# Attention's group norm: squares about the group's mean on ScalarE in place of VectorE's statistics

## The chip, the cores and the metric

The kernel runs on one core of a Trainium2 chip. The metric is the time of one execution on the device in microseconds, the median of several runs. The traces come from single executions, recorded by the hardware profiler.

## The reference

The whole program is four layers on images `x` of 32 x 192 x 56 x 56 in fp32; each layer adds its result to `x`. The change touches the first layer only, an attention with 49 "agent" tokens for each image, in six heads, on a group-normed input:

```python
def _gn(v, G=32, eps=1e-5):            # groups of 6 channels
    g = v.reshape(B, G, C // G, H, W)
    m = mean(g, axis=(2, 3, 4)); s = var(g, axis=(2, 3, 4))
    return ((g - m) / sqrt(s + eps)).reshape(v.shape)

# layer 0, on _gn(x)
qkv = xf @ Wqkv + bqkv                              # q, k, v; 3136 tokens, 192 channels
agent = q in 7 x 7 blocks of 8 x 8 pixels, averaged  # 49 tokens
agent_attn = softmax(agent * scale @ k^T + pos_bias) # over the 3136 tokens
agent_v = agent_attn @ v
q_attn = softmax(q * scale @ agent^T + agent_bias)   # over the 49 agents
out = (q_attn @ agent_v + depthwise_conv3x3(v)) @ proj_w + proj_b
x = x + out
```

The other three layers (a two-way recurrent scan, a shift with a 3 x 3 filter, a long convolution through spectra) come after it and are not changed.

## The kernel before

`all_blocks` builds a filter for the last layer (`make_filter`), runs `attention` image by image, then `scan_pairs` and `channel_blocks`. Attention takes the first 4,990 us of the profiled execution.

An image lies in SBUF as two tiles with channels in the partitions: `x[0]` holds channels 0 to 127 as 128 x 3136, and `x[1]` holds the other 64 channels as 128 x 1568, the upper half of the picture in partitions 0 to 63 and the lower half in 64 to 127. The picture is cut into `NK` = 4 vertical strips of `WIDTHS` 16, 16, 16 and 8 columns; `j` counts strips.

The loop over images has two halves. In the first half, for each strip, `weigh` makes agents' scores (L659, L660), their negative maximum `low` on VectorE (L661) and their exp on ScalarE (L663); `turn_v`, `turn`, `gather` and `settle` transpose and sum them with v; `find_v` makes v for a later strip, `convolve` its depthwise filter on VectorE (eight L646 for each of two tiles). With the last strip, `moments` of the *next* image is called. In the second half, `join` combines the strips (L724 to L739). Then `ask(j)` scores pixels against agents (products L751 and L752, maximum L755, difference L756, exp L764 on ScalarE, row sums L766 to L768), `turn_back` transposes the result (L778) and ScalarE copies it out of PSUM as `pqT` (L782), `answer` multiplies by the agents' values (L791, L796, added by L793 and L797), and `project` multiplies by `proj_w` (L911 to L924) and adds to the image (L806, L812), with a square for the next layer's norm (L819). These are staggered over `t`:

```python
for t in range(1, NK + 2):
    if t < NK:            asked[t] = ask(t, gq)
    if more and t == 1:   mean, d = spread_of(mv)
    if more and t == 2:   rs, nb = scaling(mean, d, pools); normed(nxt, rs, nb, 0)
    if t <= NK:           back[t - 1] = turn_back(t - 1, asked[t - 1])
    ...
    if t >= 2:            project(t - 2, done[t - 2], x, st)
    if t <= NK:           answer(t - 1, back[t - 1], values, done[t - 1])
```

The norm of the next image is spread over these steps. `moments` takes, on VectorE, seven `bn_stats` of 448 elements for `x[0]` (L512) and four of 392 for `x[1]` (L514), two aggregates (L516, L517) that give mean and variance of each partition, then sums of eight neighbours `by_x` (L521) and from those the 7 x 7 block sums `pool_a` and `pool_c` (L524 to L535). `grouped` forms sums over the six channels of a group with four small TensorE products (L542). `spread_of` gets the group's mean from them and `d`, the partition's variance plus the square of its distance from the group's mean. `scaling` takes the group's mean of `d`, makes `rs` and `nb` (Ln and Exp on ScalarE, L560 and L561), and scales the block sums. `normed` writes the normed strips (L599, L603) and `find_agents` makes the agents from the block sums (L575).

All PSUM work in attention uses one pool of four tiles of two banks; a product that begins a new tile waits for the reader of the one that it takes. `pr` (L662) and `pqT` (L781) share five buffers with the tag `weights`. The order of instructions on each engine is made by the scheduler of the framework when the program is built, not by the order of the source alone; on the chip each engine goes through its own list in order.

Of the kernel before, what the change touches and what calls it, by code (L numbers as in the profile page):

```python
# [20 lines left out]
F32 = mybir.dt.float32  # L21
I32 = mybir.dt.int32
AF = mybir.ActivationFunctionType
ALU = mybir.AluOpType
AX = mybir.AxisListType
# [5 lines left out]
S = 56  # L31
N = S * S
CH = 448
# [8 lines left out]
AG = 49  # L42
POOL = 7
PAIR = 2 * AG
# [189 lines left out]
def make_filter(ctx: ExitStack, tc: tile.TileContext, a, consts, filt, lags, spans, taps, beside):  # L234
# [9 lines left out]
    FE, FO = a["L3_conv_W1T"].shape  # L244
    P2 = KS * KS
    RC = 5
    n = RC * KS

    def load(name, shape, ap):
# [4 lines left out]
    w1 = load("w1", [FE, FO], a["L3_conv_W1T"])  # L254
    z = load("z", [FE, P2], a["L3_conv_z"].rearrange("b c h w -> (b c) (h w)"))
    ws = load("ws", [128, 128 + C + 4], a["filter_w"])
# [4 lines left out]
    dist = load(  # L261
        "dist", [T, P2], a["L3_conv_distance_map"].rearrange("a b h w -> (a b h w)").partition_broadcast(T)
    )
# [174 lines left out]
def attention(ctx: ExitStack, tc: tile.TileContext, a, ready, x1, st_a, st_c, beside):  # L438
# [9 lines left out]
    nc = tc.nc  # L448
    NB = x1.shape[0]
    cp = ctx.enter_context(tc.tile_pool(name="a_c", bufs=1))  # L450
    wp = ctx.enter_context(tc.tile_pool(name="a_w", bufs=2))
# [3 lines left out]
    UP, LOW = slice(0, 64), slice(64, 128)  # L455
    HALVES = ((0, UP), (1, LOW))
    P2 = slice(0, PAIR)

    def psum():
        return pp.tile([128, 2, BANK], F32, name="ps", tag="ps")  # L460
# [30 lines left out]
    def small(name, shape):  # L491
        return sp.tile(shape, F32, name=name, tag=name)
# [13 lines left out]

    def moments(x):

        st_a, st_c = small("st_a", [128, 7, 6]), small("st_c", [128, 4, 6])
        flat = [t.rearrange("p y x -> p (y x)") for t in x]  # L510
        for i in range(7):
            nc.vector.bn_stats(st_a[:, i], flat[0][:, i * 448 : (i + 1) * 448])  # L512
        for i in range(4):
            nc.vector.bn_stats(st_c[:, i], flat[1][:, i * 392 : (i + 1) * 392])  # L514
        mv = small("mv", [128, 2, 2])
        nc.vector.bn_aggr(mv[:, 0], st_a.rearrange("p a b -> p (a b)"))  # L516
        nc.vector.bn_aggr(mv[:, 1], st_c.rearrange("p a b -> p (a b)"))  # L517
        pool_a, pool_c = small("pool_a", [128, AG]), small("pool_c", [65, AG])
        by_x = [wp.tile([128, n, POOL], F32, name="by_x", tag=f"by_x{n}", bufs=1) for n in (S, S // 2)]
        for t in range(2):  # L520
            nc.vector.tensor_reduce(  # L521
                by_x[t].rearrange("p y q -> p (y q)"), x[t].rearrange("p y (q x) -> p (y q) x", x=8), AX.X, ALU.add
            )
        nc.vector.tensor_reduce(  # L524
            pool_a.rearrange("p (w q) -> p w q", w=POOL), by_x[0].rearrange("p (w y) q -> p w q y", y=8), AX.X, ALU.add
        )
        fours = small("fours", [64, 2 * POOL, POOL])
        for h, r in HALVES:
            nc.vector.tensor_reduce(
                fours[:, h * POOL : (h + 1) * POOL], by_x[1][r].rearrange("p (w y) q -> p w q y", y=4), AX.X, ALU.add  # L530
            )
        nc.vector.tensor_tensor(
            pool_c[0:64].rearrange("p (w q) -> p w q", w=POOL), fours[:, 0::2], fours[:, 1::2], ALU.add
        )
        nc.vector.memset(pool_c[64:65], 1.0)  # L535
        return mv, (pool_a, pool_c)

    def grouped(src):
        ps = psum()
        for t in range(2):  # L540
            for s in range(2):
                mm(ps[:, 0, t : t + 1], norm4[:, 2 * s + t], src[s], start=(s == 0), stop=(s == 1))  # L542
        return ps[:, 0, 0:2]

    def spread_of(mv):

        mean = small("mean", [128, 2])
        nc.vector.tensor_copy(mean, grouped([mv[:, t, 0:1] for t in range(2)]))
        d = small("d", [128, 2])
        nc.vector.tensor_tensor(d, mv[:, :, 0], mean, ALU.subtract)  # L550
        nc.vector.tensor_tensor(d, d, d, ALU.mult)
        nc.vector.tensor_tensor(d, d, mv[:, :, 1], ALU.add)
        return mean, d

    def scaling(mean, d, pools):
# [95 lines left out]
    def weigh(j, g, low, sums):  # L651
        _, n, _ = sizes(j)
        prs = []
        for p in range(3):
            cols = slice(p * PAIR, (p + 1) * PAIR)
            ps = psum()
            for h in range(2):
                px = slice(h * n, (h + 1) * n)
                mm(ps[P2, h, :n], g[:, cols], xs_a[j][:, px], start=True, stop=False)  # L659
                mm(ps[P2, h, :n], gk_c[0:KC, 2 * j + h, cols], xs_c[j][0:KC, px], start=False, stop=True)  # L660
            nc.vector.tensor_reduce(low[:, j, p : p + 1], ps[P2, :, :n], AX.XY, ALU.max, negate=True)  # L661
            pr = wp.tile([PAIR, 2, CH], F32, name="pr", tag="weights", bufs=5)  # L662
            nc.scalar.activation(  # L663
                pr[:, :, :n], ps[P2, :, :n], AF.Exp, bias=low[:, j, p : p + 1], accum_out=sums[:, j, p : p + 1]
            )
            prs.append(pr)
        return prs
# [103 lines left out]
    def turn_back(j, pq):  # L771
        _, n, ns = sizes(j)
        out = []
        for p in range(3):
            ps = psum()
            for q in range(2 * ns):
                h, s = divmod(q, ns)
                nc.tensor.transpose(  # L778
                    ps[P2, h, s * SUB : (s + 1) * SUB], pq[:, q, p * PAIR : (p + 1) * PAIR], ident[:SUB, :SUB]
                )  # L780
            t = wp.tile([PAIR, 2, CH], F32, name="pqT", tag="weights", bufs=5)  # L781
            nc.scalar.copy(t[:, :, :n], ps[P2, :, :n])  # L782
            out.append(t)
        return out
# [38 lines left out]

    nxt = ready.first
    mv, pools = moments(nxt)
    rs, nb = scaling(*spread_of(mv), pools)
    ag = find_agents(0, pools)
    gk = seen(ag, wkT, gk_c, "gk_a")
    for j in range(NK):
# [3 lines left out]
    for b in range(NB):  # L833
        x, more = nxt, b + 1 < NB
        if more:
            nxt = ready.image(nc, a, b + 1)
        beside(b)
        low, sums = small("low", [PAIR, NK, 3]), small("sums", [PAIR, NK, 3])
        got = sp.tile([PAIR, NK, C], F32, name="got", tag="got", bufs=1)
        turned, asked, back = {}, {}, {}  # L840
        for j in range(NK):
            prs = weigh(j, gk, low, sums)
            if j == 0:
                gq = seen(ag, wqT, gq_c, "gq_a")
            vT = turn_v(j, v[j])
            if j > 0:
                halves = gather(j - 1, *turned[j - 1])
            if j + 2 < NK:
                v[j + 2] = find_v(j + 2)
            turned[j] = turn(j, prs), vT  # L850
            if j > 0:
                settle(j - 1, halves, got)
            if j + 1 < NK:
                o[j + 1] = convolve(j + 1)
            elif more:
                mv, pools = moments(nxt)
        halves = gather(NK - 1, *turned[NK - 1])
        asked[0] = ask(0, gq)
        settle(NK - 1, halves, got)
        values = join(low, sums, got)  # L860
        done, o = o, {}
        st = small("st", [128, 2, 9])
        for t in range(1, NK + 2):
            if t < NK:
                asked[t] = ask(t, gq)
            if more and t == 1:
                mean, d = spread_of(mv)
            if more and t == 2:
                rs, nb = scaling(mean, d, pools)
                normed(nxt, rs, nb, 0)  # L870
            if t <= NK:
                back[t - 1] = turn_back(t - 1, asked[t - 1])
            if more and t in (3, 4):
                v[t - 3] = find_v(t - 3)
            if t >= 2:
                project(t - 2, done[t - 2], x, st)
            if t <= NK:
                answer(t - 1, back[t - 1], values, done[t - 1])
            if more and t == 2:
                ag = find_agents(b + 1, pools)  # L880
                normed(nxt, rs, nb, 1)
            if more and t == 3:
                gk = seen(ag, wkT, gk_c, "gk_a")
                normed(nxt, rs, nb, 2)
            if more and t == 4:
                o[0] = convolve(0)
                normed(nxt, rs, nb, 3)
        nc.sync.dma_start(out=st_a[:, b % 2, b // 2], in_=st[:, 0])
        for h, r in HALVES:
            nc.sync.dma_start(out=st_c[b % 2, :, h, b // 2], in_=st[r, 1])  # L890
        nc.sync.dma_start(out=x1[b, 0:128], in_=x[0].rearrange("p y x -> p (y x)"))
        for h, r in HALVES:
            nc.sync.dma_start(
                out=x1[b, 128:C, 1568 * h : 1568 * h + 1568], in_=x[1][r].rearrange("p y x -> p (y x)")
            )
# [1082 lines left out]
```

## Time and profile before

| | |
|---|---|
| median of 3 runs | 10,783.73 us (10,777.28 to 10,800.41) |
| the profiled execution | 10,811.08 us, its span 10,809.3 us |
| granted TensorE clock, mean of the span | 0.95 |
| busy of the span: TensorE, VectorE, ScalarE, GpSimd | 89%, 86%, 59%, 27% |
| attention, join of the first image to join of the last (L727) | 256.4 to 4,910.8 us, 31 intervals |
| join to join, images 2 to 23 | 150.0 to 151.6 us |
| L512, 224 executions | 0.61 us (median) |
| L514, 392 elements | 0.55 us |
| L819, 896 elements with its sum | 1.04 us, and 0.19 to read the sum |

Times in traces are counted from the start of the span. In the timelines a row has start, length, engine, line and operation, the tiles it writes and reads with partitions x elements, and how many like rows were put together; in brackets stands how long the engine sat idle before it and what ended that. L12 is line 12 of the kernel before. PE is TensorE, PEld its weight loads, DVE VectorE, ACT ScalarE, POOL GpSimd, SP SyncE. The windows view gives busy time of each engine in a stretch, the clock that TensorE was granted there (1.00 is full), and the DMA engines' share.

### The profile page before, as it was taken

How to read it: one execution, taken by the hardware profiler on the slowest of the kernel's cores; microseconds unless marked ns; L12 is line 12 of the kernel's file. 1: busy time of each engine (PE TensorE's matmuls, PEld its weight loads, DVE VectorE, ACT ScalarE, POOL GpSimd, SP SyncE). 2: the span in 40 equal slices, each digit the busy share in tenths (PEclk: the TensorE clock that was granted, in tenths of full speed). 3: DMA queues.
4: the chain of work that ended last, by engine and by line, in shares of the span. 5: the costliest groups of instructions: out<-in, count | busy, mean ns of one | idle time of the engine just before them, and what ended most of it. 6: DMA issues, size and time to landing. Idle time of an engine off the chain costs nothing. (4 is left out here: it accounts for less than half of the span.)

```text
span 10809.3 us, 166766 instructions
## 1 busy us (share of the span) xinstructions
PE 9604.3 (89%) x64806; PEld 5959.0 (55%) x64806; DVE 9260.0 (86%) x11668; ACT 6372.8 (59%) x11964; POOL 2918.0 (27%) x2614
## 2 busy tenths in 40 slices
PE   6999999999999999998888888888888799999998
PEld 3555555555555555554333333333333577787876
DVE  5888888888888888887999999999999577777877
ACT  3555555555555555554666666666666466666766
POOL 0000000000000000002655555555555444444441
PEclk8999999999999999998999999999999899999999
DMA  4211221112121111111344333333444589999998
GB/s 122 63 47 49 63 64 63 37 58 63 64 63 35 61 46 46 46 34 56 92 102 98 97 97 97 97 97 97 97 101 103 153 269 273 274 275 273 278 274 264
DMA packets 1104877, 1240.31 MB, mean 115 GB/s; under 512 B 773091, under 2 KB 807200, under 8 KB 1091992
## 3 DMA queue, kind: packets, MB, share of 16 engines
q1 hardware_dynamic: 1083148, 1201.53, 38.8%
q10 hardware_dynamic: 20932, 28.02, 1.0%
q8 instruction: 516, 8.45, 0.3%
q14 instruction: 281, 2.30, 0.1%
HBM read 915.94 MB, written 306.43 MB: 113 GB/s over the span
## 5 line engine op out<-in xcount | busy, mean ns | idle before, releaser
L646 DVE SCALAR_TENSOR_TENSOR o<-v_a,att_w,o 128x896 f32<-128x896 f32 (+1 forms) x1024 | 1053.3, 1029 | 421.7 <-ACT v_a L620 296.6
L1163 POOL MEMSET f<- 128x1 f32 x96 | 8.8, 98 | 4842.7 <-DMA st_c<-st 4837.7
L1543 DVE STREAM_TRANSPOSE z<-turned 128x1792 f32<-128x1792 f32 x192 | 677.4, 3528 | 258.3 <-ACT turned L1543 257.8
L1543 ACT COPY y<-ps 64x252 f32<-64x252 f32 (+1 forms) x2304 | 784.0, 340 | 157.9 <-PE ps L1543 128.1
L1156 ACT ACTIVATE q<-q 128x784 f32<-128x784 f32 x384 | 328.3, 855 | 813.6 <-DVE q L1151 638.5
L663 ACT ACTIVATE pr<-ps,low 98x896 f32<-98x896 f32 (+1 forms) x384 | 352.3, 918 | 567.8 <-DVE low L661 567.8
L911 PE MATMUL ps<-sq,fixed 128*128 128x392 f32 x512 | 296.8, 742 | 427.7 <-ACT sq L1234 427.7
L764 ACT ACTIVATE pq<-pq 112x1176 f32<-112x1176 f32 x224 | 265.3, 1184 | 683.3 <-DVE pq L756 654.1
L751 PE MATMUL ps<-gq_a,xs_a 128*112 128x294 f32 x1792 | 609.0, 422 | 46.6 <-DVE pq L756 24.1
L1543 POOL TENSOR_TENSOR xn<-x,scale 128x896 f32<-128x896 f32 x192 | 328.4, 1711 | 1192.3 <-DMA x<-x 759.4
L646 DVE SCALAR_TENSOR_TENSOR o<-v_c,att_w,o 128x448 f32<-128x448 f32 (+1 forms) x1024 | 634.3, 619 | 7.5 <-ACT v_c L631 2.4
L659 PE MATMUL ps<-xs_a,gk_a 128*98 128x448 f32 (+1 forms) x1536 | 638.9, 497 | 0.0
L660 PE MATMUL ps<-xs_c,gk_c 125*98 125x448 f32 (+1 forms) x1536 | 631.3, 492 | 0.0
L911 PE MATMUL ps<-x,weights 128*128 128x392 f32 x1536 | 573.7, 516 | 31.1 <-DVE bv L1185 14.1
L752 PE MATMUL ps<-gq_c,xs_c 125*112 125x294 f32 x1792 | 581.4, 411 | 0.0
L1543 PEld LDWEIGHTS ps<-toep,y 128*32 128x32 f32 x16896 | 508.2, 151 | 113.4 <-ACT y L1543 109.2
L1543 PE MATMUL ps<-toep,y 128*32 128x112 f32 x16896 | 554.8, 287 | 0.0
L1543 PE MATMUL ps<-rows,xn 128*112 128x112 f32 x3072 | 378.5, 281 | 159.6 <-POOL xn L1543 136.0
L1543 ACT ACTIVATE turned<-ps,rs 128x448 f32<-128x448 f32 (+1 forms) x576 | 384.4, 668 | 203.4 <-PE ps L1543 195.7
L1543 PE MATMUL ps<-fixed,padded 128*128 128x168 f32 x3072 | 490.0, 314 | 0.0
L766 DVE TENSOR_REDUCE sm<-pq 112x24 f32<-112x1176 f32 x224 | 307.7, 1374 | 181.9 <-ACT pq L764 181.9
L1543 PEld LDWEIGHTS ps<-fixed,padded 128*128 128x128 f32 x3072 | 455.6, 195 | 2.4 <-issue 1.9
(367 smaller groups left out, 25548.6 us busy)
## 6 DMA issues: line engine op xcount, KB each, us to landing
toep<-spans SPq DMA_DIRECT2D x192, 2352.0 KB
x<-x SPq DMA_DIRECT2D x576, 392.0 KB
x<-x SPq DMA_DIRECT2D x896, 196.0 KB
out_x<-done SPq DMA_DIRECT2D x384, 196.0 KB
spans<-lags SPq DMA_DIRECT2D x24, 2352.0 KB
x<-in_x SPq DMA_DIRECT2D x32, 1568.0 KB
x<-x SPq DMA_DIRECT2D x32, 1568.0 KB
x<-in_x SPq DMA_DIRECT2D x64, 392.0 KB
```

What stands on the lines that cost most here:

```text
L646: nc.vector.scalar_tensor_tensor(dst, tap(i), dww[:, t, i : i + 1], dst, ALU.mult, ALU.add)
L659: mm(ps[P2, h, :n], g[:, cols], xs_a[j][:, px], start=True, stop=False)
L660: mm(ps[P2, h, :n], gk_c[0:KC, 2 * j + h, cols], xs_c[j][0:KC, px], start=False, stop=True)
L663: nc.scalar.activation(pr[:, :, :n], ps[P2, :, :n], AF.Exp, bias=low[:, j, p : p + 1], accum_out=sums[:, j, p : p + 1])
L751: mm(ps[:SUB, i, :HA], xs_a[j][:, px], g, start=True, stop=False)
L752: mm(ps[:SUB, i, :HA], xs_c[j][0:KC, px], gq_c[0:KC, 2 * j + (q + i) // ns], start=False, stop=True)
L764: nc.scalar.activation(flat, flat, AF.Exp)
L766: nc.vector.tensor_reduce(sm, rows, AX.X, ALU.add)
L911: mm(out, aa, srcs[t][h], start=True, stop=False)
L1156: nc.scalar.activation(den, den, AF.Ln)
L1163: nc.gpsimd.memset(s, 0.0)
L1543: return lambda *args, **kw: self.tc.keep_in_program_order(do(*args, **kw))
```

## The change

The statistics instructions leave `moments`. It sums `by_x` once more to get each partition's sum (`mv`). `spread_of` now takes the image as well: it scales the sums to means, gets the group's mean, and has ScalarE take squares of the image about it, six activations of 784 elements, each with its sum in `parts`. VectorE adds the parts and scales them to `d`. The squares themselves are not used; they are written to buffers of the `weights` tag. `scaling`, `normed` and what follows are as before. The first image, whose norm is made ahead of the loop, takes the same path.

```diff
+    WB = 5
 def moments(x):
-        st_a, st_c = small("st_a", [128, 7, 6]), small("st_c", [128, 4, 6])
-        flat = [t.rearrange("p y x -> p (y x)") for t in x]
-        for i in range(7):
-            nc.vector.bn_stats(st_a[:, i], flat[0][:, i * 448 : (i + 1) * 448])
-        for i in range(4):
-            nc.vector.bn_stats(st_c[:, i], flat[1][:, i * 392 : (i + 1) * 392])
-        mv = small("mv", [128, 2, 2])
-        nc.vector.bn_aggr(mv[:, 0], st_a.rearrange("p a b -> p (a b)"))
-        nc.vector.bn_aggr(mv[:, 1], st_c.rearrange("p a b -> p (a b)"))
-        pool_a, pool_c = small("pool_a", [128, AG]), small("pool_c", [65, AG])
+        pool_a, pool_c, mv = small("pool_a", [128, AG]), small("pool_c", [65, AG]), small("mv", [128, 2])
...
             nc.vector.tensor_reduce(
                 by_x[t].rearrange("p y q -> p (y q)"), x[t].rearrange("p y (q x) -> p (y q) x", x=8), AX.X, ALU.add
             )
+            nc.vector.tensor_reduce(mv[:, t : t + 1], by_x[t].rearrange("p y q -> p (y q)"), AX.X, ALU.add)
...
-    def spread_of(mv):
-
-        mean = small("mean", [128, 2])
-        nc.vector.tensor_copy(mean, grouped([mv[:, t, 0:1] for t in range(2)]))
-        d = small("d", [128, 2])
-        nc.vector.tensor_tensor(d, mv[:, :, 0], mean, ALU.subtract)
-        nc.vector.tensor_tensor(d, d, d, ALU.mult)
-        nc.vector.tensor_tensor(d, d, mv[:, :, 1], ALU.add)
+    def spread_of(x, mv):
+
+        for t in range(2):
+            nc.vector.tensor_scalar(mv[:, t : t + 1], mv[:, t : t + 1], 1.0 / (N // (1 + t)), None, ALU.mult)
+        mean, away = small("mean", [128, 2]), small("away", [128, 2])
+        nc.vector.tensor_copy(mean, grouped([mv[:, t : t + 1] for t in range(2)]))
+        nc.vector.tensor_scalar(away, mean, -1.0, None, ALU.mult)
+        parts, d = small("parts", [128, 6]), small("d", [128, 2])
+        for i in range(6):
+            t, y = (0, 14 * i) if i < 4 else (1, 14 * (i - 4))
+            sq = wp.tile([128, 2 * CH], F32, name="sq", tag="weights", bufs=WB)
+            nc.scalar.activation(
+                sq[:, : 14 * S], x[t][:, y : y + 14].rearrange("p y x -> p (y x)"), AF.Square, bias=away[:, t : t + 1],
+                accum_out=parts[:, i : i + 1],
+            )
+        nc.vector.tensor_reduce(d[:, 0:1], parts[:, 0:4], AX.X, ALU.add)
+        nc.vector.tensor_reduce(d[:, 1:2], parts[:, 4:6], AX.X, ALU.add)
+        for t in range(2):
+            nc.vector.tensor_scalar(d[:, t : t + 1], d[:, t : t + 1], 1.0 / (N // (1 + t)), None, ALU.mult)
         return mean, d
...
-    rs, nb = scaling(*spread_of(mv), pools)
+    rs, nb = scaling(*spread_of(nxt, mv), pools)
...
-                mean, d = spread_of(mv)
+                mean, d = spread_of(nxt, mv)
```

More of the change, by code (lines that the diff above doesn't have):

```diff
@@ L661, in weigh @@
             nc.vector.tensor_reduce(low[:, j, p : p + 1], ps[P2, :, :n], AX.XY, ALU.max, negate=True)
-            pr = wp.tile([PAIR, 2, CH], F32, name="pr", tag="weights", bufs=5)
+            pr = wp.tile([PAIR, 2, CH], F32, name="pr", tag="weights", bufs=WB)
             nc.scalar.activation(
@@ L780, in turn_back @@
                 )
-            t = wp.tile([PAIR, 2, CH], F32, name="pqT", tag="weights", bufs=5)
+            t = wp.tile([PAIR, 2, CH], F32, name="pqT", tag="weights", bufs=WB)
             nc.scalar.copy(t[:, :, :n], ps[P2, :, :n])
```

## The prediction

> **What bounds the kernel now.** I read the page first, then the windows of the attention stage (0 to 4,990 us of 10,809), then the timelines of TensorE, ScalarE and VectorE over the fourth image (I call its times t below).
>
> ```profile
> PE 9604.3 (89%) x64806; PEld 5959.0 (55%) x64806; DVE 9260.0 (86%) x11668; ACT 6372.8 (59%) x11964; POOL 2918.0 (27%) x2614
> 716.00:866.00 150.00, 142.00 (x807) 87.11 (x806) 127.99 (x194) 80.95 (x145) 0.00 (x0) 0.98 0.18 57
> 733.00:735.00 2.00, 1.80 (x8) 1.78 (x8) 2.00 (x4) 0.00 (x0) 0.00 (x0) 0.50 0.00 0
> 735.00:740.00 5.00, 4.81 (x29) 4.41 (x30) 4.98 (x8) 3.37 (x4) 0.00 (x0) 0.59 0.00 0
> 740.00:750.00 10.00, 10.00 (x46) 6.29 (x42) 8.03 (x14) 2.60 (x3) 0.00 (x0) 1.00 0.01 2
> ```
>
> In the windows the columns are length, busy PE, PEld, DVE, ACT, POOL, then granted clock. TensorE is busy 142 of 150 us in an image: it sets the period, and an edit in attention counts only where it makes TensorE wait more or less. ScalarE is busy 81. After a wait of 3 us the clock is 0.50, and back at 1.00 near t 739.
>
> TensorE waits in two places of this image. The first is in weigh(2) and the second among the asks:
>
> ```profile
> 695.58 2.24 PE L706 MATMUL ps<-prT,vT 112*64 112x98 f32 x48 [0.58 <-ACT pr L663]
> ...
> 733.20 1.84 PE L542 MATMUL ps<-mv,att_k 128*128 128x1 f32 x8 [3.08 <-DVE pq L756]
> 735.23 4.36 PE L778 MATMUL ps<-att_k,pq 112*98 112x112 f32 x24 [0.19 <-DVE pq L756]
> 739.52 1.72 PE L791 MATMUL ps<-pqT,values 98*64 98x448 f32 x8
> 741.08 0.92 PE L796 MATMUL ps<-pqT,values 98*64 98x448 f32 x4
> 741.93 0.75 PE L751 MATMUL ps<-gq_a,xs_a 128*112 128x294 f32 x2
> ```
>
> The chain to keep in mind is exp of ask(1) (L764), the three pqT copies (L782), answer(0) (L791, L796), ask(2) (L751): TensorE runs its list in order, so ask(2) cannot start before answer(0), nor that before the copies.
>
> ```profile
> 736.97 0.91 ACT L782 COPY pqT<-ps 98x896 f32<-98x896 f32 x1 [0.61 <-PE ps L778]
> 738.47 0.91 ACT L782 COPY pqT<-ps 98x896 f32<-98x896 f32 x1 [0.59 <-PE ps L778]
> 739.63 0.91 ACT L782 COPY pqT<-ps 98x896 f32<-98x896 f32 x1 [0.26 <-PE ps L778]
> 740.43 1.19 ACT L764 ACTIVATE pq<-pq 112x1176 f32<-112x1176 f32 x1
> ...
> 762.32 1.03 ACT L819 ACTIVATE o<-x,st 128x896 f32<-128x896 f32 x1
> 763.25 0.18 ACT L819 ACTIVATION_READ_ACCUMULATOR o<-x,st 128x1 f32 x1
> 763.35 0.65 ACT L819 ACTIVATE o<-x,st 128x448 f32<-128x448 f32 x1
> ```
>
> The copies run before the second exp of ask(1). The L819 rows price a square with a sum: 1.03 us from start to start for 896 elements.
>
> VectorE has no idle time from t 663.9 to 740.1, and the statistics lie inside:
>
> ```profile
> 680.30 1.67 DVE L512 BATCH_NORM_STATS2 st_a<-x 128x6 f32<-128x448 f32 x3
> ...
> 706.95 1.94 DVE L514 BATCH_NORM_STATS2 st_c<-x 128x6 f32<-128x392 f32 x4
> ...
> 709.19 3.35 DVE L521 TENSOR_REDUCE by_x<-x 128x392 f32<-128x3136 f32 x1
> ```
>
> **The change, part by part.** The order of each engine's list is fixed when the program is built, so I take it from the built program. TensorE's, POOL's and SP's lists keep their order instruction for instruction. Three things move.
>
> *VectorE.* Eleven bn_stats and two aggregates go: 1.59 us for three (680.30 to the next start, 681.89) and 4.35 for the rest (704.31 to 709.19 less one L661 of 0.53): 5.9 us. The three small operations of d (L550 to L552) go too, 0.15 each. Two sums over by_x come. The nearest rows are L524, also 392 elements (0.83, 0.76 from start to start), and L529 (0.49 for 196): 1.25 us. About eight operations of one or two columns come at 0.07 to 0.16. In the busy stretch this is 4.5 us less; the rest falls where VectorE will wait anyway.
>
> But the list also moves the long by_x (3.28 us from start to start) from behind the last L661 to before the L661 of weigh(2), where the three statistics of 1.59 were. These three reductions come 1.7 us later, exp L663 with them, and so does the L706 that waited 0.58 for exp. No cover is left there: TensorE +1.7.
>
> From then on TensorE's own list sets the pace. The first L755 needs ask(0)'s first pair, whose last product ended near t 715.1; the 0.22 wait before 712.85 goes, so it is ready at 715.1 + 1.7 - 0.2 = 716.6. VectorE gets there near 713.5 and waits. It started L755 at 717.55, so of 4.5 us saved 1.0 is left on the path. Everything on VectorE up to ask(1) comes 1.0 earlier.
>
> *ScalarE.* Six squares of 784 elements: 1.03 less 112 elements. Between L819's rows of 896 and 448 (1.03 and 0.65) an element costs 0.85 ns, so 0.94 us each, 5.6 in all (bounds: 5.1 by L1156, 784 elements without a sum at 0.855; 6.2 by 1.03). I take 5.6, the nearest operation. ScalarE has 69 idle us an image, but the built list puts all six between the second exp of ask(1) and the three copies, in every image. The squares wait for -mean, which VectorE writes behind the row sum L766 of that exp. So: the last L756 of ask(1) ends at 738.45 - 1.0 = 737.45; exp to 738.65; VectorE is free at 740.08 - 1.0 = 739.1; L766 (1.3) to 740.4; -mean 740.55; squares to 746.25; copies end at 747.2, 748.0 and 748.8 instead of 737.9 to 740.5. Behind the squares stand the copies, and behind those answer(0), ask(2) and VectorE's list, which has four small operations on the sums of squares before L793. The buffers: the squares take "weights" buffers whose readers, the transposes of weigh, are long done, so 0.
>
> *TensorE.* Transposes of turn_back(0) are done near t 738; then it has nothing for 9 us. L791 starts at 747.25, its second operand at 748.05, ask(2) at 750.05 at full clock.
>
> *The clock.* After 3.08 us of waiting the clock was half from 733 to about 739.1, 5.9 us of running work. After 9 us I take the same 5.9, until about 753.1: L791 and L796 end at 752.0 instead of 750.05, and ask(2) loses 0.6 more, so it stands as if begun at 752.6 instead of 741.93, +10.6. Bounds: 0 (no half clock) and 5. [...]
>
> *Given back.* In the old timeline L778 waited 1.00 and L911 0.23 for copies behind ask(2); ask(2) now runs at TensorE's pace with ScalarE waiting for it, so I take 1.2 back. The group's scaling comes later by about as much as TensorE does: rs, nb and the first xs_a near t 766, pools near 768, against L575 at 770 and find_v at 778. This hides, with 1 to 2 us to spare.
>
> Sum for this image: +10.6 - 1.2 = +9.4 on a period of 150.1 (join to join), 159.5. The first 24 images average 151.3, as some have a second short half-clock stretch which I don't expect to stay: +8.0 each, 192. The last seven take 147.0 on average: there TensorE's list (both kernels) finishes ask(0)'s first pair 1.9 earlier, so 157.6 after, +10.6 each, 74.
>
> *The start.* The first image's statistics ran while the filter was made. Its by_x waits until t 160.0, where it is today; the sums, mean, squares, and scaling now follow it: 165.1 + 2.9 (sums, pools) + 2.5 (products, mean at half clock, L542 1.84) + 5.8 + 0.8 + 2.8 + 0.7 = 180.6, where L575 starts at 167.17 now: +13.
>
> Total 192 + 74 + 13 = 279. The profiled execution took 10,811.1 (span 10,809.3), 27 above the median of the three runs, 10,783.7: median after 11,063, profiled 11,090. I put 11,060.
>
> **Rivals.** *Faster:* VectorE's saving decides. It is saturated before the asks, TensorE's waits at 712.85 to 733.20 (0.22, 0.86, 0.68, 3.08) are all put down to it, ScalarE is 59% busy. If squares hide, each image gains 4.5: -140, 10,645. This decides if the squares run before the asks' exps or beside a wait of ScalarE (9.09 us before 735.18). Against it: -mean stands behind L766 in the list. *Slower by less:* no half clock and more of VectorE's 4.5 kept: +2 to +6 an image, 10,860 to 10,970. *Slower by more:* scaling doesn't hide, find_agents waits 2 to 4: 11,130 to 11,180. *Cancelled:* wait and saving balance within 0.2%, about what measurement can tell. That the statistics stay is no rival: the list has none.
>
> **How the numbers follow.** Forecast, 10,970 to 11,130: 0.66. Less: 0.19. More: 0.08. Faster: 0.04. Cancelled: 0.03. The range leaves out the faster and cancelled cases, the lower half of "less" and the top of "more": 10,920 to 11,160. Faster 0.04, same 0.03, slower 0.93.
>
> **What would show it.** After: L791 waits 8 to 10 us for copy L782 in each image; clock 0.50 behind it; six squares of 0.94 in a row ahead of the copies; L706 waits about 2.2 rather than 0.58; first L755 waits for TensorE; join to join near 159. Wrong would be: copies ahead of the squares, or TensorE busy share as before.

## The result and the profile after

The changed kernel took 11,112.8 us (median of four runs, 11,078.0 to 11,120.6) against 10,781.1 of the kernel before (10,777.3 to 10,800.4): 1.0298 times the time, 95% interval 1.0278 to 1.0318. The forecast of 11,060 was 53 short, the range of 10,920 to 11,160 held, and "slower" was the sign. The profiled execution was the quickest of the four: 11,078.0 us, with a span of 11,076.2 and a mean granted clock of 0.939, where the profile of before had 10,811.1, 10,809.3 and 0.950. All readings of the trace below are of that execution; lines of the changed code stand four further down than in the prediction (L778 is now L782, L791 is L795, L755 is L759).

The page's first part (busy time of each engine, its share of the span, instructions):

```profile
PE 9639.7 (87%) x64806; PEld 5959.6 (54%) x64806; DVE 9144.5 (83%) x11444; ACT 6541.1 (59%) x12348; POOL 2924.8 (26%) x2614
```

VectorE lost 115 us of work and 3 points of its share, ScalarE took 168 more, and TensorE's share fell from 89 to 87%. So the span grew in TensorE's waits and in slower products, not in VectorE's or ScalarE's load. The timeline of TensorE around the asks (start, duration, instruction; in brackets the idle time before it and what ended it):

```profile
773.80 1.05 PE L535 MATMUL ps<-mv,att_k 128*128 128x1 f32 x8 [2.98 <-DVE pq L760]
788.61 3.30 PE L795 MATMUL ps<-pqT,values 98*64 98x448 f32 x7 [7.71 <-ACT pqT L786]
792.40 1.75 PE L800 MATMUL ps<-pqT,values 98*64 98x448 f32 x3
794.08 1.25 PE L755 MATMUL ps<-gq_a,xs_a 128*112 128x294 f32 x2
805.44 0.98 PE L782 MATMUL ps<-att_k,pq 112*98 112x112 f32 x8 [0.28 <-ACT pqT L786]
```

This is the same image as in the prediction. On TensorE's list its times lie 43.6 us later behind weigh(2), so ask(2), at 741.93 before, would start at 785.5; it starts at 794.08, 8.6 late. TensorE reaches the mean's products (L535) 3.0 early, as VectorE, which it waits for there, is earlier. From there to the start of answer(0) (L795) it loses 8.5, nearly all of it in one bracket, the 7.71 before L795, and from there to ask(2) another 3.1, in slower products. Before the change answer(0) waited for nothing. The old wait ahead of the mean's products, 3.08, is still there with 2.98. The page's list of the costliest groups has the same wait over the whole run (busy us, mean ns of one | idle us, releaser):

```profile
L795 PE MATMUL ps<-pqT,values 98*64 98x448 f32 (+1 forms) x1024 | 264.6, 597 | 247.4 <-ACT pqT L786 247.4
```

247.4 us is 8.0 for each of the 31 images that have a next one; for most of the trace it alternates between 7.71 and 8.47. What ScalarE and VectorE did meanwhile, from their timelines:

```profile
779.08 1.19 ACT L768 ACTIVATE pq<-pq 112x1176 f32<-112x1176 f32 x1 [2.12 <-DVE pq L760]
782.07 0.95 ACT L549 ACTIVATE sq<-x,away 128x784 f32<-128x784 f32 x1 [1.80 <-DVE away L544]
786.75 0.93 ACT L549 ACTIVATE sq<-x,away 128x784 f32<-128x784 f32 x1
787.68 2.48 ACT L786 COPY pqT<-ps 98x896 f32<-98x896 f32 x3
780.59 1.37 DVE L770 TENSOR_REDUCE sm<-pq 112x24 f32<-112x1176 f32 x1
781.88 0.16 DVE L544 TENSOR_SCALAR away<-mean 128x2 f32<-128x2 f32 x1
```

The second exp of ask(1) (L768) ends at 780.27. ScalarE's next instruction is the first square, which needs -mean, and VectorE writes that behind the row sum L770. The first and the last of the six squares are shown: from 782.07 to 787.68 they take 5.61 us, and the copies that TensorE wants come behind them. The windows of TensorE's clock (window, length, busy PE, PEld, DVE, ACT, POOL, granted clock, DMA share, GB/s):

```profile
776.00:781.00 5.00, 4.72 (x24) 4.01 (x23) 4.98 (x8) 2.15 (x2) 0.00 (x0) 0.50 0.00 2
781.00:786.00 5.00, 0.00 (x0) 0.00 (x0) 2.74 (x5) 3.93 (x9) 0.00 (x0) 0.50 0.00 0
786.00:791.00 5.00, 2.39 (x7) 0.96 (x9) 0.56 (x4) 4.16 (x7) 0.00 (x0) 0.50 0.00 0
791.00:796.00 5.00, 5.00 (x15) 2.08 (x12) 1.71 (x2) 0.00 (x0) 0.00 (x0) 0.59 0.01 3
```

TensorE does nothing from 781 to 786 and runs at half clock until about 795, 6.5 us behind the start of answer(0). Where the wait is 8.47 it is 4.2 us, and in the mean of the 31 images 5.3.

### The profile page after: what moved, and what is told of

It is laid out like the page before. It is cut to its first block, busy times and chain, and to the rows that moved or that the text cites. A ratio compares the mean times of both kernels' runs of the same rounds, so it can differ in the third digit from the quotient of the medians.

```text
span 11076.2 us, 167169 instructions
## 1 busy us (share of the span) xinstructions
PE 9639.7 (87%) x64806; PEld 5959.6 (54%) x64806; DVE 9144.5 (83%) x11444; ACT 6541.1 (59%) x12348; POOL 2924.8 (26%) x2614
## 5 line engine op out<-in xcount | busy, mean ns | idle before, releaser
L768 ACT ACTIVATE pq<-pq 112x1176 f32<-112x1176 f32 x224 | 265.8, 1186 | 894.7 <-DVE pq L760 894.6
L667 ACT ACTIVATE pr<-ps,low 98x896 f32<-98x896 f32 (+1 forms) x384 | 352.4, 918 | 622.2 <-DVE low L665 622.0
L663 PE MATMUL ps<-xs_a,gk_a 128*98 128x448 f32 (+1 forms) x1536 | 638.8, 497 | 0.0
L755 PE MATMUL ps<-gq_a,xs_a 128*112 128x294 f32 x1792 | 600.2, 420 | 0.0
L759 DVE TENSOR_REDUCE mx<-ps 112x12 f32<-112x588 f32 x448 | 340.4, 766 | 244.1 <-PE ps L756 244.1
L795 PE MATMUL ps<-pqT,values 98*64 98x448 f32 (+1 forms) x1024 | 264.6, 597 | 247.4 <-ACT pqT L786 247.4
```

The costliest lines, as they stand in the source:

```text
L667: nc.scalar.activation(pr[:, :, :n], ps[P2, :, :n], AF.Exp, bias=low[:, j, p : p + 1], accum_out=sums[:, j, p : p + 1])
L755: mm(ps[:SUB, i, :HA], xs_a[j][:, px], g, start=True, stop=False)
L759: nc.vector.tensor_reduce(mx, by_head, AX.X, ALU.max)
L768: nc.scalar.activation(flat, flat, AF.Exp)
L795: mm(ps[r, h, :n], values[:, p], pqT[p][:, h, :n], start=True, stop=True)
```

## The experiments

Theory 1, that of the prediction: the place of the squares in ScalarE's list makes TensorE wait for the copies behind them. Rival 2: VectorE's new order (by_x ahead of the maxima of weigh(2)) costs. Rival 3: ScalarE's extra 5.6 us an image cost wherever they stand. The kernel before ran beside each group with medians of 10,792.6 to 10,794.4 us; ratios are to those runs.

**The two halves of the change, apart.** The first kernel is the kernel before with the squares added, unread; the second is the changed kernel without squares.

```diff
 # first: the kernel before, in spread_of
         nc.vector.tensor_copy(mean, ...)
+        nc.vector.tensor_scalar(away, mean, -1.0, None, ALU.mult)
+        for i in range(6):
+            ...
+            nc.scalar.activation(sq[:, : 14 * S], ..., AF.Square, bias=away[:, t : t + 1], accum_out=parts[:, i : i + 1])
 # second: the changed kernel, in spread_of
-        for i in range(6): ...                      # squares
-        nc.vector.tensor_reduce(d[:, 0:1], parts[:, 0:4], AX.X, ALU.add)
-        nc.vector.tensor_reduce(d[:, 1:2], parts[:, 4:6], AX.X, ALU.add)
+        nc.vector.tensor_tensor(d, away, away, ALU.mult)
```

> The kernel before with its bn_stats, its aggregates and its d kept, plus -mean and six squares of 784 elements that nobody reads, at the place where the changed kernel has them (behind the second exp of ask(1), ahead of the three pqT copies; -mean behind the row sum of that exp). Theory 1 (mine: the place of the squares in ScalarE's list makes TensorE wait): nearly all of the loss without any of VectorE's change. The copies come 8 to 9 us later, and the 2.2 us an image that VectorE's shorter list gave back in the changed kernel are missing: +9.5 an image (8.5 to 10.5) over 31 images, +6 at the start, 11,085 us (11,030 to 11,130); answer(0) waits 8 to 10 us for a copy, then half clock. Rival 2 (VectorE's order, by_x ahead of the maxima of weigh(2), is what costs): no change, 10,780. Rival 3 (ScalarE's load as such, 5.6 us an image wherever it stands): 10,955.

> The changed kernel without its six squares and their sums: d is (-mean) squared, so the scale of each image is not that of the reference; VectorE's part of the change (pooled sums instead of statistics) stays whole, and the built list has the three copies at their old place, ahead of the second exp of ask(1). It prices VectorE's saving alone. Theory 1: the first maximum of ask(0) comes 2.2 us earlier against TensorE's list, so does ask(1), so 2 us an image: 10,725 us (10,680 to 10,760). Rival 'VectorE's saving decides': 4.5 us an image, 10,645. Rival 2 (VectorE's order costs): about 11,000 or more, as the squares are no part of it. Rival 3 (ScalarE's load): 11,113 less 174, 10,940.

Measured: with unused squares 11,145.1 us, ratio 1.0328 (1.0311 to 1.0345), 15 above the top of my range; without squares 10,764.5, ratio 0.9971 (0.9959 to 0.9984), 4 above it. The two halves multiply to the whole: 1.0328 x 0.9971 = 1.0298. So the squares cost 351 us (11,145.1 less 10,794.4; and 11,112.8 less 10,764.5 is 348), and VectorE's part of the change, new order included, gains 30. That ends rival 2, and with it "VectorE's saving decides": with no square at all the gain is 30, not 140. Rival 3's 174 us is half of the price. TensorE's timeline with the unused squares (L800 is answer(0) there, L787 turn_back):

```profile
761.67 1.70 PE L787 MATMUL ps<-att_k,pq 112*98 112x112 f32 x8 [0.31 <-DVE pq L765]
771.09 3.30 PE L800 MATMUL ps<-pqT,values 98*64 98x448 f32 x7 [7.72 <-ACT pqT L791]
```

The same wait, to a hundredth, in a kernel that has all of the old statistics. Without squares the same place reads as follows (L774 is turn_back, L787 answer(0)): answer(0) follows at once, and only the old wait is left, with 2.98.

```profile
740.10 1.84 PE L535 MATMUL ps<-mv,att_k 128*128 128x1 f32 x8 [2.98 <-DVE pq L752]
742.13 4.69 PE L774 MATMUL ps<-att_k,pq 112*98 112x112 f32 x24 [0.19 <-DVE pq L752]
746.75 1.78 PE L787 MATMUL ps<-pqT,values 98*64 98x448 f32 x8
```

**The same six squares at other places.** Only the call is moved.

```diff
             if t < NK:
                 asked[t] = ask(t, gq)
-            if more and t == 1:
-                mean, d = spread_of(nxt, mv)
 # late: behind turn_back(0), in the same loop
                 back[t - 1] = turn_back(t - 1, asked[t - 1])
+            if more and t == 1:
+                mean, d = spread_of(nxt, mv)
 # between: behind ask(0)
         asked[0] = ask(0, gq)
+        if more:
+            mean, d = spread_of(nxt, mv)
 # early: behind the pooled sums
                 mv, pools = moments(nxt)
+                mean, d = spread_of(nxt, mv)
```

> The changed kernel with the call that makes mean and squares moved behind turn_back(0) in the source. The same six squares, of the same size; the built list now has them behind the three pqT copies and the second exp of ask(1), ahead of the first exp of ask(2), where ScalarE stood idle for 7.4 us in the kernel before. Theory 1: copies and answer(0) return to their old place, the squares hide, and VectorE's 2 us an image are kept, less up to 1 where VectorE waits for the sums of squares between two maxima of ask(2): 10,740 us (10,680 to 10,800). Rival 3 (load): 11,110, no change from the changed kernel. Rival 2 (VectorE's order, which is the same here up to ask(1)): 11,080 to 11,110.

> The changed kernel with the call that makes mean and squares moved directly behind ask(0) in the source: the mean's products ahead of ask(1), the squares behind the two exps of ask(0) and ahead of the three copies and the first exp of ask(1), where ScalarE stood idle for 9.1 us. Theory 1: the squares hide there too, TensorE keeps its pace: 10,740 us (10,670 to 10,800). Rival 3 (load): 11,110. Rival 2 (VectorE's order): 11,080 to 11,110.

> The changed kernel with the call that makes mean and squares moved further forward, directly behind the pooled sums and ahead of the last gather and of ask(0). The built list has the six squares ahead of the last copy of halves (which TensorE's transposes of settle wait for) and of the first exp of ask(0), and the sums of squares ahead of VectorE's first maximum of ask(0). Theory 1 (what stands behind the squares decides, not their load): squares from 1 us behind the join for 5.6 us; the maximum, ready 4.3 us behind the join, now comes at about 7, 2.4 later, the exp with it, and the transposes of settle 5 later: +2.4 to +4 an image against the squares behind ask(0) (10,690), +75 to +125: 10,790 us (10,750 to 10,830). Rival (the earlier the mean and the squares, the better): 10,690 or less. Rival 3 (load): as the squares behind ask(0), 10,690.

Measured: late 10,812.1 us, ratio 1.0015 (1.0003 to 1.0027); between 10,689.5, ratio 0.9898 (0.9881 to 0.9915); early 10,870.0, ratio 1.0072 (1.0056 to 1.0089). One and the same load costs 348 us above no squares in the changed kernel, 48 here in "late", and in "between" the kernel is even quicker than without squares: rival 3 is out. The call that is moved holds the mean's products too, so for "late" and "early" the 48 and the loss are those of the whole call; for "between" the two are taken apart below. Two of the three sizes were missed.

Late is 12 above my range. Its base was missed by 40 (no squares gave 10,764.5, not 10,725), and against that base the squares cost 48 and not 15. The joins of the trace stand 149.5 us apart against 148.7 without squares, which is 27 over 31 images (half clock is 9.4 us an image in the mean for 7.5, and half of that difference is 0.9, an estimate that would cover it). The first join comes 7.4 later, and what follows the last one takes 13.8 longer, in stages that the move does not touch; the three make the 48 by which the two profiled executions differ.

Early is 40 above the range, by the predicted mechanism with a larger size. ScalarE's copy of halves, TensorE's ask(0) and VectorE's first maximum, from the three timelines:

```profile
731.69 0.38 ACT L712 COPY halves<-ps 128x294 f32<-128x294 f32 x1
732.12 0.75 PE L755 MATMUL ps<-gq_a,xs_a 128*112 128x294 f32 x2 [2.38 <-ACT halves L712]
734.40 0.77 DVE L759 TENSOR_REDUCE mx<-ps 112x12 f32<-112x588 f32 x1 [2.24 <-PE ps L756]
```

The copy stands behind the squares. ask(0) itself, not only the transposes of settle, waits for it: its next product needs the PSUM tile that the copy empties. So the first maximum comes 8.4 us behind the join (725.96) instead of 4.3, 4.1 late where I had taken 2.4. The joins stand 6.1 us further apart than in "between" (152.2 to 146.1 in the mean). Half clock, which the forecast had left out, has a large part in that: 10.0 us an image for 2.9, of which half, 3.6, is lost, as an estimate.

Between fell in its range, 50 below the single figure, but no place can gain what squares cost, and it is 75 below no squares at all. TensorE's timeline and windows there:

```profile
734.83 0.94 PE L782 MATMUL ps<-att_k,pq 112*98 112x112 f32 x8 [1.39 <-DVE pq L760]
736.82 2.90 PE L782 MATMUL ps<-att_k,pq 112*98 112x112 f32 x16 [1.05 <-ACT pqT L786]
```

```profile
736.00:741.00 5.00, 4.18 (x22) 3.13 (x24) 4.68 (x8) 3.99 (x5) 0.00 (x0) 0.66 0.00 0
741.00:746.00 5.00, 5.00 (x24) 2.88 (x21) 4.12 (x5) 0.80 (x1) 0.00 (x0) 1.00 0.01 3
```

The wait of 2.98 is gone. Waits of 1.39 and 1.05 are in its place, and the clock is half for one stretch of 3.4 us only. Over the 31 images half clock is 7.5 us an image in the mean without squares and 2.9 with squares between; half of the difference, 2.3 as an estimate, is most of the 2.6 by which the joins stand closer. Besides the squares, the mean's products differ: they stand ahead of ask(1), not behind it. That is theory 5, tried below.

**Length of the squares, and the clock behind the wait.**

```diff
 # short: squares of one column of each 14 rows
-                sq[:, : 14 * S], x[t][:, y : y + 14].rearrange("p y x -> p (y x)"), AF.Square, ...
+                sq[:, :14], x[t][:, y : y + 14, 0], AF.Square, ...
 # warm: extra products in the wait
                 back[t - 1] = turn_back(t - 1, asked[t - 1])
+            if more and t == 1:
+                hot = psum()
+                for i in range(18):
+                    mm(hot[:98, 0, :HA], asked[0][:, 7, 0:98], asked[0][:, 7], start=True, stop=True)
```

> The changed kernel with squares of 14 elements (one column of each 14 rows) instead of 784, so the spread is not the reference's; number, place and waits of the six squares stay, only their length goes. Between the rows of 896 and 448 elements a square costs 0.85 ns an element, so one takes about 0.94 - 0.65 = 0.29 us and the six 1.7 instead of 5.6. Theory 1 (the squares stand between TensorE and its copies, one for one): answer(0) waits 3.8 us instead of 7.7, so -3.9 an image, and one or two stretches of half clock of 3.4 us fewer (1.7 each): 10,960 us (10,920 to 10,995). The 2.8 us that stay are for -mean behind its row sum. If the place only mattered through -mean and not through the squares' length: 11,080 to 11,110. If the load counted wherever it stands: 11,113 - 31 x 3.9 = 10,990.

> The changed kernel with 18 extra products of 112 rows and 294 columns on TensorE (results unread) between the transposes of turn_back(0) and answer(0), that is in the wait of 7.7 us. They take some 4.5 us at full and 9 at half clock, so they fill most of the wait without prolonging it by more than 1. It prices the half clock after the wait alone. Theory 1: answer(0) still starts when its copy is there, but at full clock, and the 6.2 us of half clock behind it go: -3.1 an image, 11,015 us (10,980 to 11,050). Rival: half clock there costs nothing, as TensorE soon waits for others anyway: 11,110, or up to 11,140 where the products run over.

Measured: short 10,969.8 us, ratio 1.0160 (1.0144 to 1.0177); warm 11,030.0, ratio 1.0223 (1.0206 to 1.0240). Both fell in their ranges.

```profile
773.40 3.30 PE L795 MATMUL ps<-pqT,values 98*64 98x448 f32 x7 [3.94 <-ACT pqT L786]
```

The short squares, 0.30 us each, leave a wait of 3.94 (3.8 expected). So up to answer(0) the squares count one for one: in the mean of the images the wait is 4.0 shorter (3.97 for 7.98). The medians are 143 us apart, 4.6 an image, as forecast. But the traced run, 11,022.8 us, is the slowest of its five, and in it the joins are only 2.3 closer (158.6 to 156.3). There the half clock behind the start of answer(0) did not shrink, as I had taken; it grew, from 5.3 us an image to 8.4, and half of that growth, 1.6 as an estimate, takes back what is missing. The four quicker runs (10,963.7 to 10,970.6) have a granted clock of 0.941 to 0.943 instead of 0.939; that they had fewer half-clock stretches fits, but none of them has a trace.

In the warm kernel first the extra products and answer(0) on TensorE's timeline, then the windows that stand beside those of the changed kernel above:

```profile
780.12 9.42 PE L880 MATMUL ps<-pq 112*98 112x294 f32 x36
789.47 1.72 PE L795 MATMUL ps<-pqT,values 98*64 98x448 f32 x8
```

```profile
776.00:781.00 5.00, 4.83 (x25) 4.20 (x24) 4.98 (x7) 1.57 (x2) 0.00 (x0) 0.52 0.00 0
781.00:786.00 5.00, 5.00 (x22) 3.35 (x21) 2.42 (x6) 4.50 (x9) 0.00 (x0) 1.00 0.00 0
786.00:791.00 5.00, 5.00 (x23) 2.69 (x23) 0.31 (x2) 3.60 (x7) 0.00 (x0) 1.00 0.01 3
```

The clock is full from 781 on, and L795 runs its products about twice as fast: 8 in 1.72 us, where the changed kernel took 3.30 for 7. Half clock fell from 17.4 us an image in the mean to 6.8. I had sized the extra products wrongly: the trace has two for each (x36), and they took 9.4 us instead of 4.5, an estimate of mine, so answer(0) starts 36.2 us behind the join instead of 34.8. Although TensorE was made to work longer than it had waited, the kernel gained 83 us, 2.7 an image; in the two traces the joins are 1.5 closer (158.6 to 157.0). With the 1.4 that answer(0) starts later, the half clock was worth some 2.9 to 4.1 an image, as an estimate; my term for it was 2.6.

**The place of the mean's products alone.** The call moved behind ask(0) as in "between", once in the kernel before, untouched otherwise, and once in the changed kernel without squares.

```diff
         asked[0] = ask(0, gq)
+        if more:
+            mean, d = spread_of(mv)        # in the loop: removed
```

> The kernel before, statistics and all, with only the call that makes mean and d moved directly behind ask(0) in the source; nothing of the change is in it. The mean's products then stand ahead of ask(1) instead of behind it. Theory 5 (for the squares behind ask(0), which were 75 us quicker than no squares at all): what was gained there is the place of the mean's products, which take a PSUM tile; without them between ask(1) and turn_back(0) TensorE's wait of 3.0 us there is split and one stretch of half clock of 3.4 us is left instead of two or three. Then the kernel before gains the same 2.4 us an image: 10,720 us (10,690 to 10,750). Rival (the gain needs the squares or the shorter list of VectorE): 10,780 to 10,800.

> The changed kernel without squares, as in the run without them (d is (-mean) squared, so the scales are not the reference's), and with the call moved directly behind ask(0). Against the run with squares at that place it prices the six squares in ScalarE's idle time ahead of ask(1). Theory 5: they cost nothing there: 10,685 us (10,665 to 10,700), the same as with squares (10,690). Rival (the squares themselves brought the gain by delaying a copy): 10,750 to 10,770, as without squares before.

Measured: the kernel before 10,724.3 us, ratio 0.9938 (0.9915 to 0.9962); no squares 10,699.6, ratio 0.9913 (0.9897 to 0.9930). What theory 5 says of the place holds: of the gain of "between", 0.6% comes from the place of the mean's products and needs nothing of the change. No squares at 0.9913 and squares at 0.9898 have overlapping intervals: behind ask(0) the six squares cost nothing that can be measured. TensorE's timeline of the kernel before with that one move (L778 is turn_back):

```profile
728.83 0.94 PE L778 MATMUL ps<-att_k,pq 112*98 112x112 f32 x8 [1.22 <-DVE pq L756]
730.76 2.55 PE L778 MATMUL ps<-att_k,pq 112*98 112x112 f32 x16 [1.00 <-ACT pqT L782]
```

As with "between", 3.08 has become 1.22 and 1.00. Half clock fell from 8.0 us an image in the mean to 3.5; half of that, 2.3 as an estimate, is nearly all of the 2.4 by which the joins came closer (150.1 to 147.8).

The reason that theory 5 gives is not shown, though. It says that the products between ask(1) and turn_back(0) make the long wait. In the late kernel they are gone from there too, to behind turn_back(0), and the wait stands whole, ahead of turn_back(0) itself (L782 there). With the call behind ask(0) and no squares it is shorter (L774 is turn_back there):

```profile
750.07 0.94 PE L782 MATMUL ps<-att_k,pq 112*98 112x112 f32 x8 [2.98 <-DVE pq L760]
731.48 0.94 PE L774 MATMUL ps<-att_k,pq 112*98 112x112 f32 x8 [1.78 <-DVE pq L752]
```

So the runs show only that it helps to have the products ahead of ask(1); whether by the PSUM tile or by work done before the wait was not tried apart. In "between" and in the kernel before with the move, VectorE's list also takes the first maximum of ask(1) ahead of the sum that makes `values`. Without squares it does not, and the gain is there all the same.

**The better version.** "Between" once more:

> The changed kernel with the call directly behind ask(0), once more, with more rounds, as the version to be recommended: 10,690 us (10,670 to 10,705), 0.9898 of the kernel before (0.988 to 0.9915). If the first measurement was luck: above 10,720.

Measured: 10,682.1 us (10,659.9 to 10,692.9), ratio 0.9901 (0.9884 to 0.9917). It beats the kernel before by 1.0% and the changed kernel by 3.9% (10,682.1 against 11,112.8). Its page:

```profile
PE 9514.9 (89%) x64806; PEld 5872.8 (55%) x64806; DVE 9117.9 (86%) x11444; ACT 6542.3 (61%) x12348; POOL 2886.5 (27%) x2614
```

ScalarE does as much as in the changed kernel (6,541), in a span that is 418 us shorter.

## Why the prediction was right, step by step

**ScalarE's list, the step that carried it: right.** Six squares in a row ahead of the copies, 5.61 us for a forecast of 5.6. Only the forecast wait was long: 7.7 to 8.5 for "8 to 10". ask(2) starts 8.6 to 9.4 late, by whether the two traces are laid over each other behind weigh(2) or ahead of it; the forecast, counted from ahead of it, was an equivalent of 10.6, with 0.6 for the clock behind its start. The difference of 1.2 is VectorE's, in the next paragraph.

**VectorE's part: right in kind, mis-sized in two terms.** In weigh(2) the late by_x costs 0.9 and not 1.7 (TensorE's times lie 42.7 later ahead of the wait and 43.6 behind it): the exps come later, yet the wait for them now falls on a transpose, where 1.24 has taken the place of 0.58, and the product that I expected to wait 2.2 waits no more:

```profile
738.29 0.87 PE L682 MATMUL ps<-att_k,v 128*112 128x128 f32 x6 [1.24 <-ACT pr L667]
739.09 2.24 PE L710 MATMUL ps<-prT,vT 112*64 112x98 f32 x48
758.11 0.77 DVE L759 TENSOR_REDUCE mx<-ps 112x12 f32<-112x588 f32 x1 [3.04 <-PE ps L756]
```

The first maximum of ask(0) waits for TensorE, as forecast, but comes 2.2 us earlier instead of 1.0. Without squares the joins stand 1.5 us closer and not 1.0, 45 over the run, and the first of them comes 13.7 later. That the medians give 30 where 31 images at 1.0 make 31 is luck: the 30 holds the later start, which the forecast counted apart.

**The half clock: right in size.** I took 5.9 us behind answer(0) from the old profile's row; in this image it is 6.5, in the mean of the 31 images 5.3 (3.8 to 6.8), and the warm kernel prices it at 2.9 to 4.1, where I had 2.6.

**Given back: right.** 1.2 forecast; the wait of 1.00 is 0.28 now, and that of 0.23 is gone, so 0.95.

**Scaling hides: right.** No wait of find_agents shows. **Start: right as far as it went.** L579 starts at 179.16 where L575 started at 167.17, +12.0 for +13. But the first join comes 18.5 later. In the first image's weigh(0) TensorE now waits 7.92 for an exp (L667, at 225.40) where it waited 2.26 (L663, at 208.10); these 5.7 us the forecast did not have.

**The sum.** This image takes 159.3 from join to join (forecast 159.5). The first 24 intervals are 158.9 in the mean (159.3), the last seven 157.5 (157.6). Over 31 intervals that is +261 for a forecast of 266, but the parts were less good: in the old trace these means are 151.7 and 144.7, not the 151.3 and 147.0 that the forecast starts from (the 24th interval is 160.5, the last 129.1), so the first 24 grew by 171 for 192 and the last seven by 90 for 74. The two profiles differ by 267 for 279: 18.5 up to the first join, the 261, and 12.4 less behind the last one. The medians differ by 332, and that is where the forecast fell 53 short. The step that failed is the last: "27 above the median", carried over from the old profile to the new one. The new profile is the quickest of its four runs and lies 35 below the median; the other three have a clock of 0.936 instead of 0.939. More half-clock stretches in those runs would explain it (0.003 of 11,100 us is 33, an estimate), but no trace of them exists, so this is only argued. Nor is it known why the later stages, whose code is unchanged, took 12.4 us less in the new profile; over the twelve traces they take 5,863 to 5,907.

**The rivals.** "Faster" priced VectorE's saving at 140 us; without squares it is 30, as TensorE sets the pace at the first maximum. "Slower by less" needed no half clock, and the windows show it; "by more" needed a wait of find_agents, and there is none.

## What to carry to other kernels

Work that was moved to an idle engine cost, in these runs, what stood behind it in that engine's list. Before moving work, find in the built order the instruction that follows it and the engine that waits for that one: here 5.6 us ahead of a copy, with the wait for -mean before them and the half clock behind, cost 11 us an image, and the same 5.6 us ahead of an exp that was late anyway cost nothing. The place of small products, like those of the mean, is worth trying: moving them alone gained 0.6%, though why was not shown. And a wait of TensorE is priced together with the half clock behind it, over many images and not one, as it differed from image to image (3.8 to 6.8 us behind the same answer(0)).

## What the runs showed of the hardware that was not expected

In these traces the half clock came in whole pieces. Summed over one image in slices of half a microsecond it was 3.4 us (between), 6.8 (before; warm), 10.2 (no squares), 13.7 (late), 17.1 (unused and short squares) and 20.5 (changed): one to six times 3.41 us (20.48 / 6 in the changed kernel). Other images of the same kernels have other multiples (in the changed kernel mostly 20.5 and 13.7 in turn), so the means over 31 images, used above, differ from these. In the late kernel two images have the same waits of TensorE (2.98 and 1.00; 2.97 and 1.00), yet the first stays at half clock for 13.7 us and the second for 3.4:

```profile
752.00:757.00 5.00, 4.99 (x26) 4.96 (x28) 3.73 (x7) 3.82 (x4) 0.00 (x0) 0.50 0.00 2
757.00:762.00 5.00, 5.00 (x14) 1.40 (x11) 4.43 (x6) 2.61 (x6) 0.00 (x0) 0.50 0.00 0
1056.00:1061.00 5.00, 5.00 (x31) 3.96 (x31) 4.31 (x7) 3.22 (x4) 0.00 (x0) 0.75 0.00 0
1061.00:1066.00 5.00, 5.00 (x22) 3.16 (x19) 4.90 (x8) 3.84 (x9) 0.00 (x0) 1.00 0.00 0
```

From 752 to 762 TensorE is busy 9.99 of 10 us and stays at 0.50. The joins of that kernel differ accordingly, 151.7 us for the first image and 147.1 for the second, so images with waits of the same length were 4.6 us apart. What decides between the two was not tried. From the 7th to the 23rd image the joins repeat in six traces, within 0.1 us, at whole multiples of 3.4133 us (317.44 / 93): every image takes 160.43 with unused squares (47 times) and 157.01 in both the short and the warm kernel (46 times), every two images 317.44 in the changed kernel (93), every four 604.16 before (177) and 597.33 in "late" (175). So the short and the warm kernel, which wait quite differently ahead of answer(0) (3.94 us and not at all), take the same time. Why the distances are such multiples was not shown. In the other six traces no such fixed distance shows.
